# Block product 5 of the first expert matrix product, split into seven half-size products, and the hidden stage run from one list of steps

## The chip, the cores and the metric

The kernel runs on one core of one Trainium2 chip. The metric is the device time of one execution in microseconds, as the median of several runs; smaller is better. A core has a matrix engine (TensorE, in the profile PE, with its weight loads as PEld), a vector engine (VectorE, DVE), a scalar engine (ScalarE, ACT), GpSimd (POOL) and SyncE (SP), the last two here mostly issuing DMAs. TensorE writes into PSUM banks; ScalarE and VectorE read them out.

## The reference

An adaptive linear layer, then a mixture of experts in which each expert picks its tokens, then a residual sum. The part that the change touches is the first of the two expert products:

```python
X_in = xt[idx]                       # 8 experts x 1024 tokens x 512
h = gelu(einsum('ekd,edh->ekh', X_in, W1) + b1[:, None, :])    # 512 -> 2048
X_e = einsum('ekh,ehd->ekd', h, W2) + b2[:, None, :]           # 2048 -> 512
out = zeros((N, D)).at[idx].add(G[..., None] * X_e)            # scattered back
```

All of it is in float32.

## The kernel before

**Stages.** After the adaptive layer and the routing (the first 180 us), the kernel works through 8 experts `e` and two halves `p` of the hidden width: 16 pairs. Each pair has a *hidden stage*, which makes `H` = gelu(X W1 + b1) for 1024 tokens and 1024 hidden columns, and an *out stage*, which multiplies `H` with W2 and scatters the rows to `out`. The first pair (0, 0) has a hidden stage of another form (`hidden_unit`), so `hidden_stage` runs 15 times. In the stage (e, 1) the token indices of the next expert are made (`indices`, line 857; `fetch`), and in the out stage of (e, 1) its tokens are transposed and summed (`prepare`, line 987).

**Seven products for eight.** Both products are made with a Strassen-Winograd scheme. Tokens and weights are cut two by two, and seven block products stand in for eight: 1 = A11 B11, 2 = A12 B21, 3 = S4 B22, 4 = A22 T4, 5 = S1 T1, 6 = S2 T2, 7 = S3 T3, with S1 to S4 sums of token blocks (`left_sums`, line 952) and T1 to T4 sums of weight blocks (`weight_sum_steps`, line 191). The block (1, 1) of the result is 1 + 2; with U2 = 1 + 6, u4 = U2 + 5 and u3 = U2 + 7, the other three are u4 + 7, u3 + 4 and u4 + 3, up to signs.

**A whole block product** in the hidden stage has 512 tokens, 256 input columns and 512 hidden columns. It is done in four units `u` of 128 hidden columns; one unit is two matmuls of 128 x 512 (line 1073) in one bank.

**A block product at the second level** is again cut two by two and made with seven smaller products (`second_level`, line 1076). It has two rounds `r` = 0, 1 (hidden columns of units r and r + 2); in each round each of its seven steps is one matmul of 128 x 256. Steps 1, 6, 5 and 3 add up in one bank "a", and after 1, 6 and 5 ScalarE copies the bank out (`snap`, line 1099) before the next step may write there; step 3 is copied out by line 1124. Steps 7 and 4 use a bank "c", read by VectorE after 5 (line 1120) and after 4 (line 1128). Step 2 uses a bank "b" of which there is one for all (line 1108). The banks "a" and "c" of a round come from one of two pairs, `ps_t` or the tag "c" of `ps_mm`. The sums for the second level are made by VectorE for all its block products at once: `weight_sums` (lines 214 to 217, operations of 128 x 1024) and `second_sums` (line 974). Their tokens and weights lie in the tiles `x_l2` and `w1_l2`.

**Before the change**, block products 2, 7, 3 and 4 are at the second level, 1, 6 and 5 whole. `three_products` (line 1181) lets 1, 6 and 5 of one unit add up in one bank, copies it out after each (line 1196, `snap1`, `snap2`, `snap4`: P1, U2, u4), and adds these to what the second level has left in `H` (lines 1199 and 1207), with a gelu by ScalarE after each block (line 1200). `hidden_stage` (line 1132) has the order of the steps written out: for each of four units a whole product 1, then two rounds `a` and `b` in turns, with 6 and 5 of the unit between their steps.

**What sets the order on the engines.** Each engine works its queue in order. The program's order is rearranged when the kernel is built, by a scheduler that follows the waits; the order is then fixed. The calls in `between` (the indices of the next expert, and the sums of W2's blocks, lines 201 to 204) are put behind a marked step, and `held` are the last two steps of the out stage before, which run inside the hidden stage that follows.

Of the kernel before, what the change touches and what calls it, by code (L numbers as in the profile page):

```python
# [11 lines left out]
F32 = mybir.dt.float32  # L12
# [8 lines left out]
P = 128  # L21
# [4 lines left out]
def tile_modulated_expert_choice_ffn(  # L26
# [15 lines left out]
    nc = tc.nc  # L42
    B, L, C = x.shape
    W = condT.shape[0]
    E, D, H = w1.shape
# [6 lines left out]
    HALF = 512  # L52
# [112 lines left out]
    U = HP // 2  # L165
    QD = D // 2
    Q = HALF // 2
    L2 = (2, 7, 3, 4)
    w1_blocks, w2_blocks = {}, {}

    def weight_blocks(kind, where, name):
# [34 lines left out]
    def weight_sums(kind, blk, name):  # L206
        for _ in weight_sum_steps(kind, blk, name):
            pass
        if kind == "w1":

            b = {(k, j): blk["l2"][:, :, k, j * Q : (j + 1) * Q] for k in range(2) for j in range(2)}
            t = fx.tile([P, 3, len(L2), Q], F32, tag="w1_sums", name=f"w1_sums_{name}")
            t1, t2, t4 = [t[:, n, :, :] for n in range(3)]
            nc.vector.tensor_add(t1, b[0, 0], b[0, 1])
            nc.vector.tensor_add(t2, t1, b[1, 1])
            nc.vector.tensor_add(t4, t2, b[1, 0])
            nc.vector.tensor_add(b[0, 1], b[0, 1], b[1, 1])
            for m, which in enumerate(L2):
                all_ = {**b, "t1": t1, "t2": t2, "t3": b[0, 1], "t4": t4}
                blk["l2", which] = {n: v[:, m, :] for n, v in all_.items()}  # L220

    def load_w1(e, ps):
        where = {}
# [114 lines left out]
    with tc.tile_pool(name="p1c", bufs=1) as p1c, tc.tile_pool(name="p1", bufs=2) as p1, \  # L338
# [344 lines left out]
        held = []  # L683
        summed = None
        for b in range(B):
# [20 lines left out]
            for u in range(2):  # L706
                with ExitStack() as held_back:
# [3 lines left out]
                    p = unit(b, u, yT)  # L711
# [6 lines left out]
                    added = p[4]()  # L718
                    held = p[5:]
# [232 lines left out]
    def left_sums(a11, a12, a21, a22, s):  # L952

        nc.vector.tensor_sub(s["s3"], a11, a21)  # L954
        nc.vector.tensor_sub(s["s1"], a22, a21)
        nc.vector.scalar_tensor_tensor(s["s2"], s["s3"], -1.0, a22, op0=ALU.mult, op1=ALU.subtract)  # L956
        nc.vector.scalar_tensor_tensor(s["s4"], s["s2"], -1.0, a12, op0=ALU.mult, op1=ALU.subtract)
# [16 lines left out]
    def second_sums(e):  # L974


        s = tokens[e][0]
        a = {(i, k): s["l2"][:, :, k, i * Q : (i + 1) * Q] for i in range(2) for k in range(2)}
        more = fx.tile([P, 2, len(L2), Q], F32, tag="x_sums", name=f"x_sums_{e}")
        s2 = {"s1": a[1, 0], "s2": more[:, 0, :, :], "s3": more[:, 1, :, :],  # L980
              "s4": fx.tile([P, len(L2), Q], F32, tag="xT10", name=f"x_s4_{e}")}
        left_sums(a[0, 0], a[0, 1], a[1, 0], a[1, 1], s2)
        for m, which in enumerate(L2):
            all_ = {**s2, "11": a[0, 0], "12": a[0, 1], "22": a[1, 1]}
            s["l2", which] = {n: v[:, m, :] for n, v in all_.items()}

    def prepare(e):

# [84 lines left out]
            nc.tensor.matmul(ps, lefts[k], rights[k], start=(start and k == 0), stop=(k == n - 1),  # L1073
                             skip_group_check=True)

    def second_level(e, p, which, r, H):


        s, blk = tokens[e][0]["l2", which], w1_blocks[e, p]["l2", which]
        name = f"{e}_{p}_{which}{r}"  # L1080
        i0, j0 = {2: (0, 0), 3: (0, 1), 4: (1, 0), 7: (1, 1)}[which]
        out = {(i, j): H[:, r + 2 * j, j0, i0 * HALF + i * Q : i0 * HALF + (i + 1) * Q]
               for i in range(2) for j in range(2)}
        st = {}

        def mm(tag, left, right, start):
            if start:
                if tag == "b":
                    t = bank("b", f"q{name}", 1)
                elif L2.index(which) % 2:  # L1090
                    t = bank("c", f"q{tag}{name}", 2)
                else:
                    t = ps_t.tile([P, HALF], F32, tag="t", name=f"ps_q{tag}_{name}")
                st[tag] = t[:, 0:Q]
            product(st[tag], [blk[right][:, r * P : (r + 1) * P]], [s[left]], start)

        def snap(n, scale=1.0):
            t = sp.tile([P, Q], F32, tag=f"osnap{n}", name=f"q{n}_{name}")
            nc.scalar.mul(t, st["a"], scale)
            return t  # L1100

        def p1():
            mm("a", "11", (0, 0), True)
            st["s1"] = snap(1)

        def p2():
            mm("b", "12", (1, 0), True)
            return nc.vector.tensor_add(out[0, 0], st["b"], st["s1"])  # L1108

        def p6():  # L1110
            mm("a", "s2", "t2", False)
            st["u2"] = snap(2)

        def p7():
            mm("c", "s3", "t3", True)

        def p5():
            mm("a", "s1", "t1", False)
            st["u4"] = snap(4, -1.0)
            nc.vector.tensor_sub(out[1, 1], st["u4"], st["c"])  # L1120

        def p3():
            mm("a", "s4", (1, 1), False)
            nc.scalar.mul(out[0, 1], st["a"], -1.0)

        def p4():
            mm("c", "22", "t4", False)
            nc.vector.tensor_add(out[1, 0], st["c"], st["u2"])

        return {1: p1, 2: p2, 3: p3, 4: p4, 5: p5, 6: p6, 7: p7}  # L1130

    def hidden_stage(e, p, H, between, held, then):

        for n, u in enumerate((0, 2, 1, 3)):
            one = three_products(e, p, u, H)
            a, b = [second_level(e, p, which, u % 2, H) for which in ((4, 3) if n % 2 else (2, 7))]
            one[1]()
            if n == 0:  # L1140
                for f in held:
                    f()
                then()
            if n % 2:
                one["c11"]()
            a[1]()
            b[1]()
            mark = a[2]()
            one[6]()
            if n % 2:  # L1150
                one["u3"]()
            b[2]()
            a[6]()
            b[6]()
            a[7]()
            b[7]()
            a[5]()
            b[5]()
            one[5]()
            a[3]()  # L1160
            a[4]()
            if n % 2:
                one["c22"]()
                for o in (first, one):
                    o["c21"]()
                b[3]()
                b[4]()
                for o in (first, one):
                    o["c12"]()
            else:  # L1170
                one["c11"]()
                b[3]()
                b[4]()
                one["u3"]()
                one["c22"]()
                first = one
            for work in between.get(n, ()):
                with tc.issue_after(mark.ins):
                    work()

    def three_products(e, p, u, H):


        s, blk = tokens[e][0], w1_blocks[e, p]
        name = f"h{e}_{p}_{u}"
        bias = [b1_sb[:, e, p * HP + j * U + u : p * HP + j * U + u + 1] for j in range(2)]
        out = {(i, j): H[:, u, j, i * HALF : (i + 1) * HALF] for i in range(2) for j in range(2)}
        st = {}
# [9 lines left out]
        def add(i, j, n, scale):  # L1198
            added = nc.vector.tensor_add(out[i, j], out[i, j], st[n])  # L1199
            nc.scalar.activation(out[i, j], out[i, j], AF.Gelu, bias=bias[j], scale=scale)  # L1200
            return added

        return {1: partial(then_snap, 1, "11", (0, 0)), 6: partial(then_snap, 2, "s2", "t2"),
                5: partial(then_snap, 4, "s1", "t1"),
                "c11": partial(add, 0, 0, 1, 1.0), "c22": partial(add, 1, 1, 4, -1.0),
                "c21": partial(add, 1, 0, 2, 1.0), "c12": partial(add, 0, 1, 4, -1.0),
                "u3": lambda: nc.vector.tensor_add(st[2], st[2], out[1, 1])}

    def hidden_unit(e, p, u, H, early=False):

# [176 lines left out]
    H = fx.tile([P, U, 2, KG * P], F32, tag="H", name="H_0_0")  # L1387
# [69 lines left out]
```

## Time and profile before

| what | value |
|---|---|
| three runs | 1697.31, 1697.42, 1697.84 us |
| median | 1697.42 us |
| profiled execution | 1692.17 us, of which its span is 1690.4 us |
| instructions | 20019 |
| one expert, from one stage to the same stage of the next expert (744.76 to 932.59 us) | 187.83 us |
| TensorE, ScalarE and VectorE busy in those 187.83 us | 187.83, 71.49 and 127.25 us |
| HBM read and written | 120.46 and 65.37 MB |

The span is what the profiler saw from the first to the last instruction of the program; the profiled execution is one run of its own, 5.25 us shorter than the median of the three others. A matmul in float32 leaves two records in the trace, so a step of the second level, one matmul in the code, is "x2" in the timeline, and one unit of a whole product is "x4". A record's duration reaches beyond the start of the next one, because matmuls overlap: the time that one costs is the distance between starts.

### The profile page before, as it was taken

To read this page: it belongs to the slowest core of one execution; us is meant where nothing else is said; L and a number is where in the kernel's file an instruction comes from. 1 tells how busy PE (TensorE), PEld (TensorE's weight loads), DVE (VectorE), ACT (ScalarE), POOL (GpSimd) and SP (SyncE) were. 2 spreads that over 40 slices of the span, in tenths; PEclk is the share of its full clock that TensorE was granted. 3 is DMA by queue.
4 is the path that set the end of the run, shared out by engine and by line. 5 is a ranking of instruction groups with operands and counts; after the bars stand their busy time and mean duration, and the time that the engine had idled before them with its cause. 6 is when DMAs were issued, how large, how long until landed. Compare 5 with 4: busy or idle time off the path is not lost.

```text
span 1690.4 us, 20019 instructions
## 1 busy us (share of the span) xinstructions
PE 1666.4 (99%) x7366; PEld 1273.3 (75%) x7366; DVE 1139.9 (67%) x2060; ACT 635.6 (38%) x1325; POOL 314.8 (19%) x238
## 2 busy tenths in 40 slices
PE   9997999999999999999999999999999999999997
PEld 5785577787868787777868787877878686877776
DVE  5885796857569565857668576846677576846561
ACT  3543323425152534335251524334251524343351
POOL 0111003120222112030222113120212023120202
PEclk9999999999999999999999999999999999999999
DMA  9724726742473226641573236542573146442403
GB/s 207 183 52 159 236 45 130 176 87 57 88 182 86 52 69 141 154 93 50 100 198 73 50 74 152 127 93 56 100 201 81 33 89 163 106 87 63 87 1 50
DMA packets 143267, 178.77 MB, mean 106 GB/s; under 512 B 16824, under 2 KB 92856, under 8 KB 143040
## 3 DMA queue, kind: packets, MB, share of 16 engines
q1 hardware_dynamic: 118240, 115.19, 24.4%
q0 software_dynamic: 24912, 62.27, 22.0%
q8 instruction: 58, 0.95, 0.2%
q14 instruction: 41, 0.34, 0.1%
q10 hardware_dynamic: 16, 0.02, 0.0%
HBM read 120.46 MB, written 65.37 MB: 110 GB/s over the span
## 4 chain that ended last, share of the span: by engine, by line
PE 94%; DVE 3%; ACT 1%; DMA 1%; issue 0%; POOL 0%; POOLq 0%; DVEq 0%; ACTq 0%
PE ps_a_o L1073 26%; PE ps_a_h L1073 19%; PE ps_c_o L1073 13%; PE ps_b_o L1073 6%; PE ps_c_qa L1073 6%; PE ps_qa L1073 6%; PE ps_b_q L1073 3%; PE ps_qc L1073 3%; PE ps_c_qc L1073 3%; PE ps_ya L81 2%; PE ps_yc L81 1%; PE ps_y L81 1%; ACT xmT L523 1%; DVE spare L786 1%; PE ps_c_h L1073 1%; PE ps_yt L750 1%
## 5 line engine op out<-in xcount | busy, mean ns | idle before, releaser
L1341 POOL DMA_INDIRECT out<-o_o,idx x128 | 227.8, 1780 | 1131.7 <-DVE o_o L1338 432.4
L1073 PE MATMUL ps_a_h<-xs,w_t 128*128 128x512 f32 x496 | 233.7, 593 | 0.0
L1199 DVE TENSOR_TENSOR H<-H,snap_h 128x512 f32<-128x512 f32 x240 | 160.2, 688 | 61.7 <-ACT snap_h L1196 58.1
L1308 ACT ACTIVATE snap_o<-ps_a_o,gain 128x256 f32<-128x256 f32 x128 | 60.3, 471 | 323.2 <-PE ps_a_o L1073 323.2
L1200 ACT ACTIVATE H<-H,b_sb 128x512 f32<-128x512 f32 x240 | 166.6, 718 | 36.2 <-DVE H L1199 36.2
L1196 ACT COPY snap_h<-ps_a_h 128x512 f32<-128x512 f32 x180 | 105.0, 583 | 167.2 <-PE ps_a_h L1073 167.2
L1073 PEld LDWEIGHTS ps_a_h<-xs,w_t 128*128 128x128 f32 x496 | 93.5, 190 | 68.8 <-issue 61.1
L1073 PE MATMUL ps_b_o<-w,H 128*128 128x256 f32 x512 | 126.6, 380 | 0.0
L1073 PE MATMUL ps_c_o<-w,hs_o 128*128 128x256 f32 x512 | 125.3, 382 | 0.0
L1073 PE MATMUL ps_a_o<-w,H 128*128 128x256 f32 x512 | 124.1, 379 | 0.0
L1073 PE MATMUL ps_a_o<-w_t,hs_o 128*128 128x256 f32 x512 | 123.3, 381 | 0.0
L1073 PE MATMUL ps_a_o<-w_t,H 128*128 128x256 f32 x512 | 121.4, 379 | 0.0
L1073 PE MATMUL ps_a_o<-w,hs_o 128*128 128x256 f32 x512 | 121.1, 379 | 0.0
L1073 PE MATMUL ps_c_o<-w_t,H 128*128 128x256 f32 x504 | 119.3, 379 | 0.0
L1073 PE MATMUL ps_a_h<-xT,w 128*128 128x512 f32 x248 | 117.1, 594 | 0.0
L1108 DVE TENSOR_TENSOR H<-ps_b_q,q 128x256 f32<-128x256 f32 x120 | 50.8, 423 | 90.7 <-PE ps_b_q L1073 66.6
L1073 PEld LDWEIGHTS ps_a_o<-w,hs_o 128*128 128x128 f32 x512 | 96.3, 190 | 20.4 <-issue 7.2
L1073 PEld LDWEIGHTS ps_c_o<-w,hs_o 128*128 128x128 f32 x512 | 95.9, 190 | 17.6 <-DVE hs_o L954 4.7
L1073 PEld LDWEIGHTS ps_b_o<-w,H 128*128 128x128 f32 x512 | 96.7, 190 | 14.9 <-DVE o_o L1319 2.0
L1073 PEld LDWEIGHTS ps_a_o<-w_t,hs_o 128*128 128x128 f32 x512 | 96.0, 190 | 15.7 <-DVE hs_o L956 3.2
L1073 PEld LDWEIGHTS ps_a_o<-w,H 128*128 128x128 f32 x512 | 97.1, 190 | 14.2 <-issue 1.1
L1073 PEld LDWEIGHTS ps_a_o<-w_t,H 128*128 128x128 f32 x512 | 97.1, 190 | 13.6 <-issue 0.5
(329 smaller groups left out, 2794.0 us busy)
## 6 DMA issues: line engine op xcount, KB each, us to landing
w<-in_w SPq DMA_DIRECT2D x78, 512.0 KB, 3.7
w_l<-in_w SPq DMA_DIRECT2D x42, 512.0 KB, 5.5
rows<-row SPq DMA_DIRECT2D x56, 260.0 KB, 3.2
xg<-rows SPq DMA_DIRECT2D x56, 256.0 KB, 5.7
x<-in_x SPq DMA_DIRECT2D x28, 256.0 KB, 8.2
y_dram<-ytok SPq DMA_DIRECT2D x5, 1024.0 KB, 4.3
w_l<-in_w SPq DMA_DIRECT2D x24, 128.0 KB, 3.6
y_dram<-ytok POOLq DMA_DIRECT2D x12, 256.0 KB, 5.1
```

The source lines that it names most:

```text
L81: behind[engine] = make()
L523: nc.scalar.mul(t, t, styles[1][:, j, b : b + 1])
L750: nc.tensor.transpose(ps[:, o * P : (o + 1) * P], yT[:, o, t * P : (t + 1) * P], ident)
L786: nc.vector.tensor_scalar(mark, ST, cand[:, c + 1 : c + 2].bitcast(F32), None, op0=ALU.is_ge, op1=ALU.add, accum_out=cnt[:, c : c + 1])
L1073: nc.tensor.matmul(ps, lefts[k], rights[k], start=(start and k == 0), stop=(k == n - 1), skip_group_check=True)
L1108: return nc.vector.tensor_add(out[0, 0], st["b"], st["s1"])
L1196: nc.scalar.copy(st[n], st["a"])
L1199: added = nc.vector.tensor_add(out[i, j], out[i, j], st[n])
L1200: nc.scalar.activation(out[i, j], out[i, j], AF.Gelu, bias=bias[j], scale=scale)
L1308: nc.scalar.mul(t, st["a"], scale)
L1341: nc.gpsimd.indirect_dma_start(out=last_rows[g] if e == E - 1 else out_rows, out_offset=bass.IndirectOffsetOnAxis(ap=idx[:, e, g : g + 1], ...
```

## The change

Three things change together.

- **Block product 5 goes to the second level.** Its sums are made apart from the other four's: three tiles `w1_sums5` and four VectorE operations of 128 x 256 for each stage, and `x_sums5` with four operations for each expert. Its result does not lie in `H` but in two tiles of 128 x 512 with the tag `snap4`.
- **The additions are rearranged.** 1 and 6 still add up in one bank (`two_products`); u4 is no longer made in the bank but by VectorE, as tile plus U2, one operation of 128 x 512 more for each unit. `add` issues each addition and gelu as soon as the products that it needs have been issued.
- **The order is one list for the whole stage.** In `ORDER` a word such as `5a6` is step 6 of block product 5 in round a (r = 0), `6.2` is the whole product 6 of unit 2, and `h` one of the two held steps of the out stage before. Ten rounds follow each other, two at a time, taking the two pairs of banks in turns (`stream`). The stage now begins with steps of 2 and 7; the loads of W2's blocks (`then`) are issued after the second `h` and not after a first whole product and both held steps.

```diff
+    ORDER = """
+        2a1 7a1 2a2 h 2a6 2a7 7a2 7a6 7a7 2a5 h 7a5 2a3 2a4 1.0 7a3 5a1 7a4 5a2 3a1
+        5a6 5a7 3a2 3a6 3a7 5a5 6.0 3a5 5a3 5a4 1.2 3a3 4a1 3a4 4a2 2b1 4a6 4a7 2b2 2b6
+        2b7 4a5 6.2 2b5 4a3 4a4 1.1 2b3 7b1 2b4 7b2 5b1 7b6 7b7 5b2 5b6 5b7 7b5 6.1 5b5
+        7b3 7b4 1.3 5b3 3b1 5b4 3b2 4b1 3b6 3b7 4b2 4b6 4b7 3b5 6.3 4b5 3b3 3b4 4b4 4b3
+    """.split()
...
+            t = fx.tile([P, 3, Q], F32, tag="w1_sums5", name=f"w1_sums5_{name}")
+            t1, t2, t4 = [t[:, n, :] for n in range(3)]
+            nc.vector.tensor_add(t1, b[0, 0], b[0, 1])
+            nc.vector.tensor_add(t2, t1, b[1, 1])
+            nc.vector.tensor_add(t4, t2, b[1, 0])
+            nc.vector.tensor_add(b[0, 1], b[0, 1], b[1, 1])
...
+        more = fx.tile([P, 3, Q], F32, tag="x_sums5", name=f"x_sums5_{e}")
+        s2 = {"s1": a[1, 0], **{f"s{n + 2}": more[:, n, :] for n in range(3)}}
+        left_sums(a[0, 0], a[0, 1], a[1, 0], a[1, 1], s2)
...
-    def second_level(e, p, which, r, H):
+    def second_level(e, p, which, r, H, stream):
...
+        if which == 5:
+            lie = [sp.tile([P, HALF], F32, tag="snap4", name=f"q5_{j}_{name}") for j in range(2)]
...
-                elif L2.index(which) % 2:
+                elif stream:
                     t = bank("c", f"q{tag}{name}", 2)
...
-        for n, u in enumerate((0, 2, 1, 3)):
-            one = three_products(e, p, u, H)
-            a, b = [second_level(e, p, which, u % 2, H) for which in ((4, 3) if n % 2 else (2, 7))]
-            one[1]()
...
+        for n, o in enumerate(ORDER):
+            ready = []
+            if o == "h":
+                held.pop(0)()
+                if not held:
+                    then()
+            elif "." in o:
+                which, u = int(o[0]), int(o[2])
+                units[u][which]()
+                left[which, u] = True
+                ready = [u]
+            else:
+                which, r, step = int(o[0]), "ab".index(o[1]), int(o[2])
+                if step == 1:
+                    inner[which, r] = second_level(e, p, which, r, H, streams % 2)
+                    streams += 1
+                mark = inner[which, r][step]() or mark
...
+            if n in place:
+                for work in between.get(place[n], ()):
+                    with tc.issue_after(mark.ins):
+                        work()
...
+            if can("11", 1, 2):
+                output(0, 0, 1)
+            if can("u4", 5, 6):
+                nc.vector.tensor_add(st[4], st[4], st[2])
+            if can("u3", "u4", 7):
+                nc.vector.tensor_add(st[2], st[2], out[1, 1])
+            if can("22", "u3"):
+                output(1, 1, 4, -1.0)
+            if can("21", "u3", 4):
+                output(1, 0, 2)
+            if can("12", "u4", 3):
+                output(0, 1, 4, -1.0)
```

More of the change, by code (lines that the diff above doesn't have):

```diff
@@ L220, in weight_sums @@
                 blk["l2", which] = {n: v[:, m, :] for n, v in all_.items()}
+            b = {(k, j): blk["t1"][:, k, j * Q : (j + 1) * Q] for k in range(2) for j in range(2)}
+            t = fx.tile([P, 3, Q], F32, tag="w1_sums5", name=f"w1_sums5_{name}")
[4 more added lines that the diff above has]
+            nc.vector.tensor_add(b[0, 1], b[0, 1], b[1, 1])
+            blk["l2", 5] = {**b, "t1": t1, "t2": t2, "t3": b[0, 1], "t4": t4}
     def load_w1(e, ps):
@@ L985, in second_sums @@
             s["l2", which] = {n: v[:, m, :] for n, v in all_.items()}
+        a = {(i, k): s["s1"][:, k, i * Q : (i + 1) * Q] for i in range(2) for k in range(2)}
+        more = fx.tile([P, 3, Q], F32, tag="x_sums5", name=f"x_sums5_{e}")
+        s2 = {"s1": a[1, 0], **{f"s{n + 2}": more[:, n, :] for n in range(3)}}
+        left_sums(a[0, 0], a[0, 1], a[1, 0], a[1, 1], s2)
+        s["l2", 5] = {**s2, "11": a[0, 0], "12": a[0, 1], "22": a[1, 1]}
     def prepare(e):
@@ L1074, in product @@
                              skip_group_check=True)
-    def second_level(e, p, which, r, H):
+    def second_level(e, p, which, r, H, stream):
         s, blk = tokens[e][0]["l2", which], w1_blocks[e, p]["l2", which]
         name = f"{e}_{p}_{which}{r}"
-        i0, j0 = {2: (0, 0), 3: (0, 1), 4: (1, 0), 7: (1, 1)}[which]
-        out = {(i, j): H[:, r + 2 * j, j0, i0 * HALF + i * Q : i0 * HALF + (i + 1) * Q]
-               for i in range(2) for j in range(2)}
+        if which == 5:
+            lie = [sp.tile([P, HALF], F32, tag="snap4", name=f"q5_{j}_{name}") for j in range(2)]
+        else:
+            i0, j0 = {2: (0, 0), 3: (0, 1), 4: (1, 0), 7: (1, 1)}[which]
+            lie = [H[:, r + 2 * j, j0, i0 * HALF : (i0 + 1) * HALF] for j in range(2)]
+        out = {(i, j): lie[j][:, i * Q : (i + 1) * Q] for i in range(2) for j in range(2)}
         st = {}
@@ L1128, in p4 @@
             nc.vector.tensor_add(out[1, 0], st["c"], st["u2"])
-        return {1: p1, 2: p2, 3: p3, 4: p4, 5: p5, 6: p6, 7: p7}
+        return {1: p1, 2: p2, 3: p3, 4: p4, 5: p5, 6: p6, 7: p7, "lie": lie}
     def hidden_stage(e, p, H, between, held, then):
-        for n, u in enumerate((0, 2, 1, 3)):
-            one = three_products(e, p, u, H)
-            a, b = [second_level(e, p, which, u % 2, H) for which in ((4, 3) if n % 2 else (2, 7))]
-            one[1]()
[L1140 to L1169, printed above, removed]
-            else:
[L1171 to L1179, printed above, removed]
@@ L1181, in three_products @@
-    def three_products(e, p, u, H):
+        units = [two_products(e, p, u, H) for u in range(U)]
+        inner, left, streams, mark = {}, {}, 0, None
+        place = [n for n, o in enumerate(ORDER) if "." in o and o[0] == "1"]
+        place = {n: m for m, n in enumerate(place)}
+        held = list(held)
+        for n, o in enumerate(ORDER):
[9 more added lines that the diff above has]
+                ready = [u]
+            else:
+                which, r, step = int(o[0]), "ab".index(o[1]), int(o[2])
[3 more added lines that the diff above has]
+                mark = inner[which, r][step]() or mark
+                todo = left.setdefault(("steps", which, r), set(range(1, 8)))
+                todo.discard(step)
+                if not todo:
+                    for u in (r, r + 2):
+                        left[which, u] = True
+                        if which == 5:
+                            units[u]["q5"](inner[5, r]["lie"][u // 2])
+                    ready = [r, r + 2]
+            for u in ready:
+                units[u]["add"](left, u)
+            if n in place:
+                for work in between.get(place[n], ()):
+                    with tc.issue_after(mark.ins):
+                        work()
@@ L1184, in three_products, with two_products @@
+    def two_products(e, p, u, H):
         s, blk = tokens[e][0], w1_blocks[e, p]
@@ L1187, in three_products @@
         out = {(i, j): H[:, u, j, i * HALF : (i + 1) * HALF] for i in range(2) for j in range(2)}
-        st = {}
+        st, done = {}, set()
         def then_snap(n, left, right):
@@ L1196, in then_snap, with output, add, can @@
             nc.scalar.copy(st[n], st["a"])
-        def add(i, j, n, scale):
-            added = nc.vector.tensor_add(out[i, j], out[i, j], st[n])
+        def output(i, j, n, scale=1.0):
+            nc.vector.tensor_add(out[i, j], out[i, j], st[n])
             nc.scalar.activation(out[i, j], out[i, j], AF.Gelu, bias=bias[j], scale=scale)
-            return added
+        def add(there, u):
+            def can(name, *needs):
+                if name in done or not all((n, u) in there or n in done for n in needs):
+                    return False
+                done.add(name)
+                return True
+            if can("11", 1, 2):
[10 more added lines that the diff above has]
+                output(0, 1, 4, -1.0)
         return {1: partial(then_snap, 1, "11", (0, 0)), 6: partial(then_snap, 2, "s2", "t2"),
[L1204 to L1207, printed above, removed]
+                "q5": partial(st.__setitem__, 4), "add": add}
     def hidden_unit(e, p, u, H, early=False):
```

## The prediction

> **What bounds the kernel now.** I read the page first: its span, busy times and chain of waits.
>
> ```profile
> span 1690.4 us, 20019 instructions
> ...
> PE 1666.4 (99%) x7366; PEld 1273.3 (75%) x7366; DVE 1139.9 (67%) x2060; ACT 635.6 (38%) x1325; POOL 314.8 (19%) x238
> ...
> PE 94%; DVE 3%; ACT 1%; DMA 1%; issue 0%; POOL 0%; POOLq 0%; DVEq 0%; ACTq 0%
> ```
>
> TensorE is busy for 99% and is 94% of the chain that ended last. Then the busy times by stage; columns after the window: its length, then busy us of PE, PEld, DVE, ACT, POOL, then clock.
>
> ```profile
> 556.93:599.98 43.05, 43.05 (x157) 29.61 (x156) 24.45 (x44) 24.36 (x54) 4.71 (x3) 1.00 0.22 43
> 462.47:506.46 43.99, 43.99 (x189) 30.33 (x188) 30.39 (x54) 24.48 (x54) 12.66 (x10) 1.00 0.75 184
> 412.15:462.47 50.32, 50.32 (x229) 43.10 (x228) 32.34 (x48) 11.33 (x23) 9.94 (x6) 1.00 0.45 95
> 506.46:556.93 50.47, 50.47 (x230) 43.02 (x229) 40.10 (x54) 11.32 (x23) 10.63 (x6) 1.00 0.43 92
> ```
>
> These are the hidden stages p = 0 and p = 1, then the out stages p = 0 and p = 1. Clock full, PE never idle for long, VectorE at 57 to 79%. The timeline gives the price of a step:
>
> ```profile
> 566.40 1.88 PE L1073 MATMUL ps_a_h<-xT,w 128*128 128x512 f32 x4
> 568.12 0.59 PE L1073 MATMUL ps_c_qa<-x_l,w_l 128*128 128x256 f32 x2
> 568.55 0.59 PE L1073 MATMUL ps_qa<-x_l,w_l 128*128 128x256 f32 x2
> 568.98 0.59 PE L1073 MATMUL ps_b_q<-x_l,w_l 128*128 128x256 f32 x2
> ```
>
> From start to start a whole unit takes 1.72 us and a second-level step 0.43: exactly a quarter. The first window holds 56 steps and 11 units, 100 step-times: 43.05 / 100 = 0.4305 us, with no gap. An out stage is 28 products of four step-times plus one early unit, 116 x 0.4305 = 49.94, so it loses 0.38 (p = 0) and 0.53 (p = 1); p = 1's hidden stage loses 0.13 beside its index matmuls (0.81). One expert loses 1.04 us in all.
>
> **The change, part by part.**
>
> *Products (TensorE).* Product 5 whole is 4 units, 16 step-times; at the second level 2 rounds of 7 steps, 14. Saved 2 x 0.4305 = 0.861 us per stage, over 15 stages **12.9 us**. This is paid in full only if TensorE stays without gaps.
>
> The page "TensorE: Matmul & The Clock Gate" of the Trainium skill, section "Back-to-back issue gap", speaks against this: in streams of weight load and matmul both set the spacing, about 81 ns for 128 columns and 131 ns for 512. My estimate from it: 98 ns for 256, 0.75 of a wide one, so 28 narrow records would cost 28 x 0.75 = 21 wide ones where 16 were, 2.1 us more per stage and 31 us over 15. The timeline above shows half a record's time for half its columns, and I go by the timeline.
>
> *Bank copies (ScalarE).* Four copies of 128 x 512 (L1196, 0.583) go; eight of 128 x 256 (L1099 and L1124, 0.38) come: +0.7 us per stage on an engine that is busy 24.4 of 43 us. Cost 0; the cover is ScalarE's idle time of 18 us.
>
> *Additions (VectorE).* Six bank readings of 128 x 256 come (starts 0.34 apart) and four u4 additions of 128 x 512 (0.60 apart): +4.4 us per stage. The new weight sums are four of 128 x 256, +1.4 per out stage, the token sums as much in every second. The hidden stage p = 1 goes to 34.8 of 43.1 us (81%), the out stage p = 1 to 42.9 of 50.5 (85%). Cost 0 while no bank is waited for; the price without that cover is the next item.
>
> *The steps' distances (waits).* How soon may a bank be written again?
>
> ```profile
> 500.00 0.59 PE L1073 MATMUL ps_b_q<-x_l,w_l 128*128 128x256 f32 x2
> 500.43 0.59 PE L1073 MATMUL ps_c_qa<-x_sums,w_sums 128*128 128x256 f32 x2
> ...
> 500.70 0.42 DVE L1108 TENSOR_TENSOR H<-ps_b_q,q 128x256 f32<-128x256 f32 x1 [1.58 <-PE ps_b_q L1073]
> ...
> 501.06 0.38 ACT L1099 ACTIVATE q<-ps_c_qa 128x256 f32<-128x256 f32 x1 [0.28 <-PE ps_c_qa L1073]
> ```
>
> ScalarE starts 0.63 us after a step's start (501.06 on 500.43) and takes 0.38, VectorE 0.70 (500.70 on 500.00) and takes 0.42; where TensorE did wait for such a copy, in the linear layer, it started 0.06 after its end (copy 91.37 + 0.56, weights at 91.99). So a bank is free 1.07 us after its step began through ScalarE, 1.18 through VectorE. I counted these distances in the changed kernel's instruction order as built. Bank "a": 3 step-times (1.29 us) at two places (2a6 to 2a5, 4b5 to 4b3), else 4 or more; margin 0.22. Bank "b": 4 at the closest (5a2 to 3a2, 4a2 to 2b2, 3b2 to 4b2), margin 0.54. Bank "c" from 7 to 4: 5 at the closest, 2.16 us against about 1.6 through both engines. None is negative. VectorE's margin is what a long operation ahead of it in its queue can use up: a W2 sum (1.13) or an index operation (1.13). Walking VectorE's queue by the distances between starts, I find each bank read 0.25 to 0.3 us before it is needed, in the W2 sums and in the index operations alike. The index matmuls now go in four groups of 8, one behind each index operation; the tightest has 0.3 us to spare.
>
> *The edges.* At the end, 12 and 21 of the last two units are added after the last step.
>
> ```profile
> 509.23 1.29 DVE L954 TENSOR_TENSOR hs_o<-H 128x512 f32<-128x512 f32 x2
> 509.98 0.70 PE L1073 MATMUL ps_c_o<-w,hs_o 128*128 128x256 f32 x2
> ...
> 514.44 1.25 DVE L993 STREAM_TRANSPOSE xT<-xg 128x1024 f32<-128x1024 f32 x1
> ```
>
> Before, the matmul that needs the first such sum comes 3.52 us after the hidden stage. Now 12 step-times (5.2 us) of other out products stand between in p = 0, and 14 (6.0) in p = 1, where a token transpose (1.16) moves ahead of the sum. VectorE's queue after the last step (one bank, two additions, one output, the transpose, the sum: 0.34 + 1.2 + 0.4 + 1.16 + 0.69 = 3.8) leaves 2.2 for backlog, and I find 2.1: the margin is gone. In the out stage of p = 1 the 2.7 us more of VectorE put two waits on TensorE, 0.15 and 0.3 by the same walk. At the start 2a6 needs the weight sums at 460.3 (before: 465.9); they were done at 449.8 and now some 1.4 later. Nothing.
>
> *Queues.* SP and POOL have the same DMAs in the same sequence. W2's loads go out behind the second held step; the sums that need them begin some 7 us earlier in the stage, at 480 where the last load was issued at 461 and lands 4 later. The index result is about 1 us later; the gathered tokens, issued until 503, land by 509 and are first needed at 518.
>
> *Sum.* -12.9 for the products. The remaining gaps I take as 1.2 us per expert against 1.04, over 7.5 experts +1.5; from below -7.8 (all gaps gone), from above +7.5 (0.5 us per stage). From the profiled execution 1692.17 - 11.4 = 1680.8. The median lies 5.25 above it, which I carry over: 1697.42 - 11.4 = **1686.0 us**, own range 1682 to 1690.
>
> **The rivals.**
>
> *Edges eat half.* The margin at the out stage's begin is about zero and VectorE is late by a transpose in seven stages (7 x 0.8) plus 0.05 per other stage: -12.9 + 6 = -6.9, **1690.5**. For it: VectorE works without a pause from 505.56 to 546 in the trace, and gets more. Against it: in that stretch TensorE lost only 0.53.
>
> *Nothing measurable.* Per stage 0.63 to 1.09 us are lost: 1694.0 to 1700.8, inside 0.2% of the median, which is about what runs of this kernel can tell from no change. It is also what comes out if the second-level rounds of 5 cost as much in gaps as they save. Middle **1697**.
>
> *Slower: a gelu at the head of ScalarE's queue.* ScalarE works in order, and a gelu (L1200, 0.72) that waits for VectorE's addition holds up every bank copy behind it; TensorE then waits for the bank. With three additions' chains (u4, u3, output) ahead of each gelu this can hit at the 4-step distances, margin 0.65. Ten rounds losing 0.15 each are 1.5 us per stage: -12.9 + 22.5 = +9.6, **1707**. It decides from 0.86 + 0.23 = 1.09 us per stage on. For it: 16 gelus per stage, each behind at least one wait. Against it: before, the same number stands between the copies, and ScalarE's copies waited only for TensorE.
>
> **How the numbers follow.** Forecast 0.73 (1682 to 1690), edges 0.12 (1690 to 1694), nothing measurable 0.07, slower 0.08. Faster by over 0.2% (below 1694.0) is the first two: 0.85; same 0.07; slower 0.08. The range 1681.5 to 1692.5 takes in the forecast and most of the edges, and leaves 0.2 out.
>
> **What would show it.** Step distance still 0.43 between starts and a hidden stage p = 0 of about 42.2 us where 43.05 were (products). 150 instead of 120 additions from bank "b"; VectorE near 1235 us busy. PE waits on ScalarE's copies by more than 10 us in total would show the slower rival, on the out stages' sums (hs_o) by more than 5 the edges. I am wrong if half the narrow steps start over 0.45 us after the one before.

## The result, and the profile after

The change makes the kernel slower by a quarter of a per cent: 1701.59 us (1698.56 to 1703.96, 8 runs) where the kernel before, on the same chip, had 1697.37 (1695.42 to 1698.43, 8 runs). The ratio is 1.0026, 95% interval 1.0015 to 1.0036. The prediction said 1686.0, 1681.5 to 1692.5, and is wrong in sign.

The page of the changed kernel: span, busy times and the chain of waits.

```profile
span 1701.4 us, 20659 instructions
...
PE 1669.6 (98%) x7546; PEld 1302.8 (77%) x7546; DVE 1232.9 (72%) x2302; ACT 644.1 (38%) x1385; POOL 323.3 (19%) x238
...
PE 91%; ACT 3%; DVE 3%; DMA 1%; issue 1%; another core or an unknown queue 0%; POOLq 0%; POOL 0%; SPq 0%; DVEq 0%; ACTq 0%
```

VectorE's 1232.9 us are close to the predicted 1235. The new thing is ScalarE, with 3% of the chain where it had 1%. The two profiled executions can't be subtracted as they stand: 7.8 of the 11 us between them arise before 211 us, in the routing and the first gather, which the change does not touch. (From the first matmul on `ps_c_h_b` to the first of `ps_a_h_a` by `xs` the profile of the kernel before has 9.5 us and that of the changed one 15.4; the kernel before without gelus, of experiment 3, has 15.1 as well.) From one expert to the same place of the next the time is 188.27 us (561.19 to 749.46) where it was 187.83.

Two hidden stages of that expert by windows, p = 0 and p = 1, each from its second word to the first product of the out stage. Columns: window, length, busy us of PE, PEld, DVE, ACT, POOL, clock.

```profile
561.19:608.45 47.26, 47.18 (x186) 34.48 (x184) 28.02 (x53) 25.83 (x59) 6.16 (x4) 1.00 0.28 57
654.03:702.88 48.85, 48.77 (x219) 35.70 (x218) 34.60 (x63) 26.32 (x60) 12.98 (x11) 1.00 0.71 172
```

The first window holds 108 step-times, the two held steps of the out stage among them: 108 x 0.4313 = 46.58, so 0.68 us are lost. The second holds 109 and the index matmuls (0.82): 47.83, lost 1.02. Before, a whole expert with its four stages lost 1.04. The clock is full (1.00), so the loss is time between steps and not slower steps.

To compare kernels I added up, over TensorE's timeline from 270 to 1635 us, the distance from each group of matmuls to the next less its number of records times 0.2157 us (256 columns; twice that for 512). I call this the lost time. It is 3.9 us before and 20.0 after. The change saved the steps and paid more than that back.

Where? The timeline of the changed kernel at the first of two places that recur in every stage:

```profile
581.01 0.59 PE L1095 MATMUL ps_qa<-x_l,w_l 128*128 128x256 f32 x2
...
581.70 1.33 ACT L1217 ACTIVATE H<-H,b_sb 128x512 f32<-128x512 f32 x2
...
582.74 0.59 PE L1095 MATMUL ps_qc<-x_sums,w_l 128*128 128x256 f32 x2
582.94 0.36 ACT L1124 ACTIVATE q<-ps_qa 128x256 f32<-128x256 f32 x1
...
583.36 0.30 PEld L1095 LDWEIGHTS ps_qa<-x_sums,w_sums 128*128 128x128 f32 x2 [0.43 <-ACT q L1124]
583.36 0.70 PE L1095 MATMUL ps_qa<-x_sums,w_sums 128*128 128x256 f32 x2
...
583.90 0.62 PE L1095 MATMUL ps_b_q<-x_l,w_l 128*128 128x256 f32 x2
```

Step 4a1 starts at 581.01. Its bank could be copied at 581.64 (0.63 after a step's start, as before the change); the copy starts at 582.94, directly after two gelus that stood ahead of it in ScalarE's queue, 1.33 us for both. Step 4a6, which needs the bank, is due at 582.74 + 0.43 = 583.17 and starts at 583.36: 0.19 lost. The step after it starts 0.54 later and not 0.43: 0.11 more. The weight load shows the wait: in steady running it starts 0.21 to 0.22 us ahead of its matmul, here both start together, and the wait is noted at the load.

The second place, 9 us on:

```profile
590.38 0.59 PE L1095 MATMUL ps_c_qa<-x_s,w_l 128*128 128x256 f32 x2
...
591.14 1.33 ACT L1217 ACTIVATE H<-H,b_sb 128x512 f32<-128x512 f32 x2
...
592.38 0.36 ACT L1149 ACTIVATE H<-ps_c_qa 128x256 f32<-128x256 f32 x1
...
592.79 0.30 PEld L1095 LDWEIGHTS ps_c_qa<-xs,w_t 128*128 128x128 f32 x2 [0.46 <-ACT H L1149]
592.79 0.70 PE L1095 MATMUL ps_c_qa<-xs,w_t 128*128 128x256 f32 x2
```

Step 2b3 at 590.38, its copy 2.00 us later behind a pair of gelus, and 5b1, the first step in that bank pair afterwards, at 592.79.

The lost time of the changed kernel by place, over 15 stages or 7 experts: step 5b1 and those after it 6.0 us, step 4a6 and the one after it 4.4; the out stages' begin, waiting for the last gelus, 2.9; the first product of the out stage's last unit at p = 1, 2.8; the index matmuls' four groups 2.3; the sums `hs_o` 1.6.

### The profile page after: what moved, and what is told of

Same layout as the page of the kernel before. It is cut to its first block, busy times and chain, and to the rows that moved or that the text cites. A ratio compares the mean times of both kernels' runs of the same rounds, so it can differ in the third digit from the quotient of the medians.

```text
span 1701.4 us, 20659 instructions
## 1 busy us (share of the span) xinstructions
PE 1669.6 (98%) x7546; PEld 1302.8 (77%) x7546; DVE 1232.9 (72%) x2302; ACT 644.1 (38%) x1385; POOL 323.3 (19%) x238
## 4 chain that ended last, share of the span: by engine, by line
PE 91%; ACT 3%; DVE 3%; DMA 1%; issue 1%; another core or an unknown queue 0%; POOLq 0%; POOL 0%; SPq 0%; DVEq 0%; ACTq 0%
PE ps_a_o L1095 25%; PE ps_a_h L1095 13%; PE ps_c_o L1095 13%; PE ps_c_qa L1095 8%; PE ps_qa L1095 7%; PE ps_b_o L1095 6%; PE ps_b_q L1095 3%; PE ps_qc L1095 3%; PE ps_c_qc L1095 3%; PE ps_ya L81 2%; ACT H L1217 1%; PE ps_yc L81 1%; PE ps_y L81 1%; ACT xmT L540 1%; DVE spare L803 1%
## 5 line engine op out<-in xcount | busy, mean ns | idle before, releaser
L1374 POOL DMA_INDIRECT out<-o_o,idx x128 | 236.9, 1851 | 1131.7 <-DVE o_o L1371 404.8
L1217 ACT ACTIVATE H<-H,b_sb 128x512 f32<-128x512 f32 x240 | 163.1, 715 | 25.4 <-DVE H L1216 22.1
L1095 PE MATMUL ps_a_o<-w,H 128*128 128x256 f32 x512 | 128.6, 381 | 0.9
L1213 ACT COPY snap_h<-ps_a_h 128x512 f32<-128x512 f32 x120 | 70.5, 587 | 148.2 <-PE ps_a_h L1095 146.5
L1095 PE MATMUL ps_a_h<-xs,w_t 128*128 128x512 f32 x256 | 124.8, 595 | 0.0
L1095 PE MATMUL ps_c_o<-w,hs_o 128*128 128x256 f32 x512 | 121.5, 380 | 0.0
L1124 ACT ACTIVATE q<-ps_c_qa 128x256 f32<-128x256 f32 x225 | 86.4, 384 | 71.5 <-PE ps_c_qa L1095 55.6
L1095 PEld LDWEIGHTS ps_c_o<-w_t,H 128*128 128x128 f32 x504 | 95.7, 190 | 13.0
L1216 DVE TENSOR_TENSOR H<-H,snap_h 128x512 f32<-128x512 f32 x120 | 79.6, 683 | 34.6 <-ACT snap_h L1213 34.6
```

The source lines that it names most:

```text
L1374: nc.gpsimd.indirect_dma_start(out=last_rows[g] if e == E - 1 else out_rows, out_offset=bass.IndirectOffsetOnAxis(ap=idx[:, e, g : g + 1], ...
```

## The experiments

Theory 1 is this list: the gain is paid back in small waits, the largest behind gelus in ScalarE's queue. Rival 2: VectorE's additions hold the banks. Rival 3: narrow steps cost TensorE more than half a whole one. Each experiment ran against the kernel before in five rounds.

| kernel | ratio to before (95%) | lost, us | ratio x 1697.4 - lost |
|---|---|---|---|
| before | 1 | 3.9 | 1693.5 |
| before, no gelus | 1.0002 (0.9993-1.0011) | 4.4 | 1693.3 |
| after | 1.0026 (1.0015-1.0036) | 20.0 | 1681.8 |
| 1 gelus behind | 0.9980 (0.9972-0.9989) | 14.2 | 1679.8 |
| 2 index together | 1.0009 (1.0000-1.0017) | 18.3 | 1680.6 |
| 3 no gelus | 0.9952 (0.9940-0.9965) | 6.9 | 1682.4 |
| 4 no sums for 5 | 1.0017 (1.0008-1.0026) | 19.4 | 1680.9 |
| 5 order held | 1.0133 (1.0118-1.0149) | 36.8 | 1683.2 |
| 6 gelus singly | 0.9966 (0.9954-0.9978) | 9.6 | 1682.0 |
| 7 = 2 + 5 + 6 | 1.0059 (1.0046-1.0073) | 24.7 | 1682.7 |
| 8 = 7, first units free | 0.9993 (0.9984-1.0002) | 15.7 | 1680.5 |
| 9 first place alone | 0.9996 (0.9987-1.0005) | 15.5 | 1681.2 |
| 10 late sums | 1.0014 (1.0005-1.0023) | 19.2 | 1680.6 |
| 11 = 2 + 6 + 10 | 0.9945 (0.9931-0.9959) | 7.1 | 1681.0 |

The last column is what a kernel would take without its lost time. It is two numbers: 1693.4 with product 5 whole and 1681.4 (mean of twelve, within 2) with product 5 split. The rest is the lost time.

**1. Gelus behind the copies.** The gelus of `output` go to a list and are issued behind the copies of 4a1 and 2b3.

```diff
-            nc.scalar.activation(out[i, j], out[i, j], AF.Gelu, bias=bias[j], scale=scale)
+            pending.append(partial(nc.scalar.activation, out[i, j], out[i, j], AF.Gelu, bias=bias[j], scale=scale))
...
+            hold = hold or o in ("5a4", "6.2")
+            if o in ("4a1", "2b3"):
+                hold = False
+                with tc.issue_after(last_copy[-1].ins):
+                    while pending:
+                        pending.pop(0)()
...
```

> The change with two pairs of gelus per hidden stage put behind the bank copy that they stood in front of on ScalarE (the copy of the bank after step 4a1, and the one after step 2b3); nothing else moves. Theory 1 (the gain was paid back by TensorE's waits for banks whose copy stands behind gelus): in the change's trace the two places lose 4.4 us (step 4a6) and 6.0 us (step 5b1) of the 20.0 us that TensorE lost between 270 and 1640 us, so the time falls by some 10 us, from 1701.6 to about 1691.5, and the lost time to about 10 us. Rival 2 (VectorE's additions hold the banks) and rival 3 (narrow steps cost TensorE more than half of a whole one): ScalarE's order does not matter, the time stays at 1701.6 within 1.5.

The time fell by 0.46%, 7.8 us. Both places are empty in its trace; instead the pair behind the copy of 2b3 stands ahead of the copy of 7b1 and another pair ahead of that of 5b1, and three steps there lose 0.1 us each. ScalarE's order matters, and where else a gelu stands matters too.

**2. Index matmuls together.**

```diff
-        for t in range(NT):
+        for t in reversed(range(NT)):
...
-                             start=(t == 0), stop=(t == NT - 1))
+                             start=(t == NT - 1), stop=(t == 0))
```

> The change with the 32 index matmuls of an expert begun with the chunk that VectorE makes last, so that all stand together. In the change they came in four groups, and TensorE lost about 0.08 us at each group, 2.3 us in seven experts. Theory 1, with this as its second part: 1701.6 - 2.3 = 1699.3, or 1.7 us of it if one of four groups' losses is left. Rivals 2 and 3: no difference, 1701.6 within 1.5. If the wait for the last chunk is longer than the steps ahead of it, the time rises instead.

Measured 1.0009, 2.9 us less, with intervals that just overlap; the lost time is 1.7 less. A group in the changed kernel, and all of them in this one:

```profile
666.54 0.35 PE L897 MATMUL ps_idx<-val,oh 128*128 128x16 bf16 x8
...
666.75 0.68 PE L1095 MATMUL ps_qa<-x_sums,w_sums 128*128 128x256 f32 x2
667.26 0.59 PE L1095 MATMUL ps_qc<-x_sums,w_t 128*128 128x256 f32 x2
```

```profile
666.06 0.97 PE L897 MATMUL ps_idx<-val,oh 128*128 128x16 bf16 x32
```

No group waited. But the step behind a group reaches to the next step in 0.51 us (666.75 to 667.26), 0.08 more than 0.43. With one group instead of four, three such losses go: 3 x 0.08 x 7 = 1.7.

**3. Both kernels without the gelus.** One line goes, in the change and in the kernel before.

```diff
-            nc.scalar.activation(out[i, j], out[i, j], AF.Gelu, bias=bias[j], scale=scale)
```

> The change without the gelus of the fifteen hidden stages (their sums go on to the second product as they are). Theory 1: both places of the first experiment are gone, 10.4 us, and of the waits at the out stages' begin (2.9 us), which are for the last gelu, some 2 us: about 1689. Rival 2 (VectorE) and rival 3 (narrow steps): these stay, at most 2 us less, 1699.5 or more.

> The kernel before without the gelus of the same fifteen hidden stages. All theories: TensorE lost 4.2 us there in all, 3.5 of it at the stages' begin and ends, so at most 3 us less, 1694.5 to 1697. Together with the run of the change without gelus it gives the price of the narrow steps alone: theory 1 and the pitch of 0.4313 us expect the change some 6 to 12 us faster once both are without gelus, rival 3 expects it no faster.

The change gains 12.5 us without its gelus, the kernel before nothing. Between the two kernels without gelus the split is worth 1699.72 - 1689.76 = 10.0 us by the medians, 8.5 by the ratios in the table. That rules out rival 3, and it shows that the gelus cost time only together with what the change brought.

**4. Without the sums for product 5.**

```diff
-            nc.vector.tensor_add(t1, b[0, 0], b[0, 1])
-            nc.vector.tensor_add(t2, t1, b[1, 1])
-            nc.vector.tensor_add(t4, t2, b[1, 0])
-            nc.vector.tensor_add(b[0, 1], b[0, 1], b[1, 1])
...
-        left_sums(a[0, 0], a[0, 1], a[1, 0], a[1, 1], s2)
```

> The change without the four additions of each weight block and the four of each expert's tokens that it needs for the seven products of product 5; the seven products use sums that lie there already in their place, so 4.4 us of VectorE per stage and 1.4 us per expert's tokens are left out and TensorE's steps stay. Theory 1 (ScalarE's order, the index matmuls, the out stage's order): the additions cost nothing, 1701.6 within 1.5. Rival 2 (VectorE's load holds the banks): their 75 us of work had to come from somewhere, so 3 us less or more, 1698.6 or below.

1.5 us less, with intervals that overlap, and the two places as they were (6.7 of the lost 19.4 directly at 5b1 and 4a6). So the new sums are not what was paid. The expectation has the work wrong: 4.4 us per stage are the bank readings and the u4 additions, which stay in. VectorE is busy for 1206.4 us where the change has 1232.9, so 26.5 us are left out of the 93.0 that the change added. For the rest of VectorE's new work see experiment 6, where all of it is there and the two places are empty.

**5. The out stage's order held.** A product that was pulled forward and then waited looked like a mistake of the scheduler.

```diff
+            if v:
+                with tc.issue_after(out_p5[e, p, v - 1].ins):
+                    mm(st["a"], "11", (0, 0), True)
...
```

> The change with two matmul groups of each out stage held back to the place that they have in the program's text: the first product of an out unit behind the fifth of the unit before it, and step 2a1 of the next hidden stage behind the last out unit's fifth product. In the change the first product of the last unit was pulled in front of two products of the unit ahead and waited 0.30 us for ScalarE's copy of its bank, and 0.11 followed: 2.8 us in seven experts. Theory 1: 1701.6 - 2.8 = 1698.8. Rivals 2 and 3: 1701.6 within 1.5. If what comes in its place waits too, no difference either, and the trace shows for what.

Slower by 18 us. The out stage's begin (p = 0) in its trace:

```profile
611.20 0.59 PE L1097 MATMUL ps_b_o<-w,H 128*128 128x256 f32 x2
...
612.17 1.56 PE L1097 MATMUL ps_b_o<-w,H 128*128 128x256 f32 x6 [0.38 <-ACT H L1223]
...
614.37 1.56 PE L1097 MATMUL ps_b_o<-w,H 128*128 128x256 f32 x6 [0.63 <-DVE o_o L1362]
```

The first wait is for the last gelus, which are late at every out stage's begin, the second for VectorE's reading of bank "b". In the change the scheduler had filled both with the second unit's first product. Holding it cost 20.2 of the lost 36.8 us.

**6. Gelus one at a time.** The list of the first experiment, with the places chosen by what TensorE does next there.

```diff
+    SLOT = {"4a1": 1, "4a6": 1, "4a5": 1, "7b1": 1, "7b6": 1, "7b5": 2, "7b3": 1}
...
+            hold = o != "5b4" and (hold or o == "5a4")
...
+            for _ in range(SLOT.get(o, 0)):
+                with tc.issue_after(last_copy[-1].ins):
+                    pending.pop(0)()
+            while pending and not hold:
+                pending.pop(0)()
```

> The change with eight of a stage's sixteen gelus issued one at a time (two at one place), each behind a bank copy that is followed by at least three narrow steps or a whole product before the next: behind 4a1, 4a6, 4a5, 7b1, 7b6, two behind 7b5, one behind 7b3. The first experiment moved two pairs and gained 7.8 us of 10.4, since its moved pair then stood before the copies of 7b1 and 5b1 (three waits of 0.1 us a stage in its trace, 4.6 us). Theory 1: without these too, the 10.4 us and no new wait, 1691.2, some 4 us below the first experiment (ratio to the kernel before 0.9964). If it is only the number of gelus ahead and not their place that counts, as in the first experiment: 1695.

Measured 0.9966 for the expected 0.9964, and the lost time is 10.4 less, all of it from the two places. The first of them in its timeline, and the same hidden stage by windows:

```profile
575.64 0.59 PE L1095 MATMUL ps_qa<-x_l,w_l 128*128 128x256 f32 x2
...
576.27 0.38 ACT L1127 ACTIVATE q<-ps_qa 128x256 f32<-128x256 f32 x1
...
576.55 0.71 ACT L1200 ACTIVATE H<-H,b_sb 128x512 f32<-128x512 f32 x1
...
577.36 0.59 PE L1095 MATMUL ps_qa<-x_sums,w_sums 128*128 128x256 f32 x2
577.80 0.59 PE L1095 MATMUL ps_qc<-x_sums,w_l 128*128 128x256 f32 x2
```

```profile
555.81:602.37 46.56, 46.56 (x186) 34.81 (x184) 27.74 (x53) 26.09 (x59) 6.61 (x4) 1.00 0.28 58
```

The copy of 4a1 starts 0.63 us after its step, one gelu fits behind it, and 4a6 starts without a wait. The stage takes 46.56 us, its 108 step-times and no more, with ScalarE as busy as in the change (26.1 and 25.8 us).

**7 and 8. All three parts.** The gelus of 6, the index matmuls of 2, and the order of 5; then with only the last unit's first product held (`if v == GH - 1:`).

> The change with the gelus of the experiment before, the index matmuls together, and the out stage's order held: all three parts of theory 1 at once. TensorE's lost time of 20.0 us less 10.4, 2.3 and 2.8 leaves 4.5 us, about what the kernel before lost (4.2), and the time is 1701.6 - 15.5 = 1686, 0.9932 of the kernel before. Rivals 2 and 3: not below 1695.

> The three parts again (gelus one at a time behind single copies, index matmuls together, order held), but of the out stage only the last unit's first product is held back, and step 2a1. When every out unit's first product was held back, TensorE waited 20 us at the begin of the second unit, since its first product had filled the wait for the stage's last gelus; that filling is left alone here. Theory 1: of the change's 20.0 us of lost time 10.4, 2.3 and 2.8 go, 4.5 are left, and the time is 1686 to 1687, 0.9935 of the kernel before. If holding anything back in the out stage costs more than it brings: above the 1689.4 that the gelus and the index matmuls alone would give.

Both missed: 7 for the reason of experiment 5, and 8 because holding the last unit's product uncovered a longer wait. The changed kernel's VectorE at that place, and TensorE and VectorE in experiment 8:

```profile
726.73 0.42 DVE L974 SCALAR_TENSOR_TENSOR x_sums<-x_sums,xs 128x256 f32<-128x256 f32 x1
727.07 1.22 DVE L974 SCALAR_TENSOR_TENSOR x_s<-x_sums,x_l 128x1024 f32<-128x1024 f32 x1
728.21 0.68 DVE L971 TENSOR_TENSOR hs_o<-H 128x512 f32<-128x512 f32 x1
728.81 0.47 DVE L1352 SCALAR_TENSOR_TENSOR o_o<-ps_b_o,gain,snap_o 128x256 f32<-128x256 f32 x1
```

```profile
722.76 1.89 PE L1097 MATMUL ps_a_o<-w,hs_o 128*128 128x256 f32 x8
...
725.42 0.48 DVE L1372 SCALAR_TENSOR_TENSOR o_o<-ps_b_o,gain,snap_o 128x256 f32<-128x256 f32 x1
...
725.95 1.35 PE L1097 MATMUL ps_b_o<-w,H 128*128 128x256 f32 x5 [1.30 <-DVE o_o L1372]
```

VectorE frees bank "b" behind a long row of token sums. In the change the scheduler had put step 2a1 and half a first product there; without them TensorE stands still for 1.46 us per expert, 10.2 in seven. The 0.30 us that I wanted back is a wait inside this filling, for ScalarE's copy of the half product's bank; with the 0.11 behind it 0.41 us are paid in place of 1.46.

**9. The first place alone.** `SLOT = {"4a1": 1, "4a6": 1, "4a5": 1}`, and nothing held after 4a5.

> The change with only the first of the two places undone: the pair of gelus in front of the copy after 4a1, and the one behind it, are issued one at a time behind 4a1, 4a6 and 4a5; the place at 5b1 stays as it is. Theory 1: the two places are separate and add up; 4.4 us of 10.4 go, from 1701.6 to 1697.2, ratio to the kernel before 0.9999, and the 6.0 us at step 5b1 stay in the trace. If the gelus are late as a whole (ScalarE has too much work there), the loss moves on to 5b1 and the time stays at 1701 to 1702.

0.9996, 5.1 us below the change, the lost time 4.5 less; 5b1 still loses its 4.2 us and the step behind it 1.5. The two places add up.

**10 and 11. Token sums later; three parts.**

```diff
-        left_sums(a[0, 0], a[0, 1], a[1, 0], a[1, 1], s2)
+    def fifth_sums(e):
...
                 work[0] = [partial(prepare, e + 1)]
+                work[GH - 1] = [partial(fifth_sums, e + 1)]
...
```

> The change with the four additions that make the token sums of product 5 for the next expert moved from the first to the last unit of the out stage of p = 1; no work is left out. In the trace VectorE works without a pause from 710.6 to 722.0 us there, these four take 1.36 us of it, and its addition that frees bank b comes 1.4 us after TensorE could have gone on; TensorE fills it with half a first product and step 2a1, and 0.41 us per expert are left. Theory 1, corrected by the two experiments that held the order (the order was a filling, the cause is VectorE's queue in this one place): 1701.6 - 2.8 = 1698.8, ratio 1.0010, and the wait of 0.3 us is gone. If the cause were the order that the scheduler chose, the 2.8 us stay: 1701.6.

> The gelus one at a time, the index matmuls together, and the token sums of product 5 moved to the last out unit: the three causes of theory 1 taken away together, none of TensorE's own work changed. TensorE's lost time of 20.0 us less 10.4, 2.3 and 2.8 leaves 4.5; the time is 1701.6 - 15.5 = 1686, 0.9932 of the kernel before (0.992 to 0.9945). Without the token sums' part 1689.4 (0.9952). Rivals: not below 1691.7, what the gelus alone gave.

Experiment 10 gained 2.0 us where 2.8 were expected, with intervals that overlap those of the change, and its lost time fell by only 0.8: bank "b" is still waited for, 0.20 us and 0.10 behind it. In its timeline the sums `hs_o` have moved up into the time that came free, ahead of the addition that frees the bank. Experiment 11 is the fastest kernel of the study: 1688.27 us, 0.9945 of the kernel before, at the upper edge of what was expected. Its page:

```profile
span 1686.1 us, 20687 instructions
...
PE 93%; DVE 3%; ACT 1%; DMA 1%; issue 1%; another core or an unknown queue 0%; POOLq 0%; POOL 0%; SPq 0%; DVEq 0%; ACTq 0%
```

ScalarE is back at 1% of the chain. TensorE's work is that of the change, record for record (x7546).

## Why the prediction was wrong

**Products: right.** A narrow step costs 0.4313 us in the changed kernel, and the kernels with the split come to 1681.4 us without their lost time against 1693.4: 12.0 us saved where 12.9 were predicted, with a scatter of 2 among the kernels. "Exactly a quarter" is not quite so: from 270 to 1635 us of both traces a record of 256 columns stands 215.8 ns from the next and one of 512 columns 429.2, so two narrow ones are 2.5 ns dearer than a wide one. At these distances the split saves 16 x 429.17 - 28 x 215.83 ns = 0.82 us per stage, 12.4 in 15. The estimate from the skill's page, by which a narrow record costs 0.75 of a wide one, does not hold for these float32 records: they cost 0.503.

**Bank copies on ScalarE, "Cost 0": the step that failed.** I took the 18 idle microseconds of the stage as the cover. The idle time is there (25.8 of 47.3 us busy), and it covers nothing where a copy stands behind two gelus and its bank is wanted again soon: what counts is when the copy gets to the head of the queue, against when TensorE comes back to the bank. The cost was 10.4 us, 0.69 per stage. With the gelus moved by a microsecond or two, at the same busy time, it is nothing (experiment 6).

**The steps' distances: counted rightly, walked on one queue only.** Bank "a" with 3 or 4 step-times is enough when the copy starts 0.63 us after the step. At 4a1 it started 1.93 after it. I walked VectorE's queue by the distances between starts and took ScalarE's copies at 0.63, from a row of the kernel before in which nothing stood ahead of the copy. Late copies were there before the change too:

```profile
579.31 0.59 PE L1073 MATMUL ps_qa<-x_l,w_l 128*128 128x256 f32 x2
...
580.05 1.33 ACT L1200 ACTIVATE H<-H,b_sb 128x512 f32<-128x512 f32 x2
...
581.29 0.37 ACT L1099 ACTIVATE q<-ps_qa 128x256 f32<-128x256 f32 x1
...
582.76 0.59 PE L1073 MATMUL ps_qa<-x_sums,w_sums 128*128 128x256 f32 x2
```

This copy starts 1.98 us after its step, behind a pair of gelus as at 4a1. It costs nothing, since the next step in its bank comes 3.45 us after the first, with a whole product between them. In the trace of the kernel before 53 of 480 such copies start 1.7 to 2.0 us after their step, and each of these banks is written again only after 3.4 us. In the changed kernel's order 4a6 and 5b1 are due five step-times after the step that they wait for, 2.16 us. So the new list did not bring the late copies; it brought the short distances behind them. The Trainium skill's page "Perfetto Trace Analysis", section "Tensor Engine Instruction (MATMUL, LD_WEIGHTS)", remarks that ACT and DVE are strict FIFO. The trace agrees: the copy that was ready at 581.64 starts at 582.94, after the second gelu.

**Additions on VectorE, "Cost 0": right in the hidden stages, within what could be measured.** Without the new sums the time is 1.5 us lower, inside the intervals; the bank readings and the u4 additions were never taken out alone. The two predicted waits of 0.15 and 0.3 us in the out stage of p = 1 are there in size, as one of 0.30 with 0.11 behind it, but by luck: it is a wait for ScalarE, and the wait for VectorE behind it is 1.46 us when nothing fills it (experiment 8).

**Index matmuls, "0.3 to spare": right on the waits, wrong on the cost.** None waited, and the four groups cost 2.3 us all the same, since each costs the next step 0.08 (the one group of the kernel before cost 0.6).

**Edges and queues.** The out stages' sums lose 1.6 us, far from the rival's 6. The wait at the out stages' begin is for the last gelus (2.9 us): without gelus it is gone from the trace (experiment 3).

**The sum.** The remaining gaps were taken as +1.5 us, from above +7.5 (1.2 against 1.04 us per expert over 7.5 experts makes +1.2; the slip of 0.3 changes nothing). They came to 20.0 - 3.9 = +16.1. With the predicted 12.9, which has the same price for a step as the lost time, that is +3.2, inside the measured interval of +2.5 to +6.1 (by the medians +4.2). The upper bound of 0.5 us per stage was too low: the stage with p = 0 alone loses 0.68.

**The rivals.** "Slower" named the mechanism, a gelu at the head of ScalarE's queue, and the point from which it decides, 1.09 us per stage; with the other losses 16.1 / 15 = 1.07 came about. It had the size wrong: ten rounds of 0.15 us, 22.5 in all, where two places cost 0.29 and 0.40 per stage, the step behind each included, 10.4 in all. What I held against it was the mistake. That ScalarE's copies waited only for TensorE before is a wrong reading, as the copy at 581.29 shows. That the same number of gelus stood between the copies is so, but the kernel before loses nothing to its gelus (experiment 3): the number says little, and the distance to the next use of the bank decides. The sign I gave for it, over 10 us of TensorE's waits on ScalarE's copies, is reached when the step behind each wait is counted in (6.2 us without it).

## What to carry to other kernels

Idle time of an engine covers a short job only if nothing long stands ahead of it in that engine's queue, or if its buffer is not wanted before both are done: for every job that hands a buffer back, walk the queue of the engine that does it, with all that else is in it, and not only the one that seems loaded, and compare with the distance to the buffer's next use. A new order of steps can make a delay count that was always there. Work that nobody waits for soon (here gelus) is best issued one piece at a time behind the jobs that hand buffers back. A product that waits in an odd place may be what is left of a longer wait: look at what it fills before you move it.

## What was not expected of the hardware

- A wait on TensorE costs more than its length: the step after it comes 0.54 us later and not 0.43, 0.11 more, at both of the places shown in the changed kernel. After the wait the weight load and its matmul start together (583.36 and 583.36); that the load is then no longer hidden behind the matmul before it is my reading of these rows, and no run tests it.
- Going over from small bf16 matmuls (128 x 16) to float32 steps costs the step behind them 0.08 us, without a wait.
